# A four-layer graph network on one core: layer 0's table first in the prologue, layer 2's sums with one-hot weights

## The chip, the core and the metric

The kernel runs on one core of a Trainium2 chip. The core has five engines, each with its own instruction queue that is worked through in order: TensorE (PE in the profile, with its weight loads as PEld), VectorE (DVE), ScalarE (ACT), GpSimd (POOL) and SyncE (SP), which here only issues transfers. Transfers run on 16 DMA engines. The time is device microseconds from start to end; each version is run several times and the median counts.

## The reference, cut

There are 12500 nodes with 128 features and 212500 edges, sorted by destination. Four layers follow one another; each normalises the nodes, applies a ReLU, gathers a row for each edge's source, works on it, and adds it up at the edge's destination.

```python
edge_index = jnp.stack([src, dst])
h = jnp.maximum(_layernorm(x, axis=-1), 0.0)
x = x + _L0_gnn_ref(h, edge_index, edge_attr_16, ...)   # attention over 4 heads
h = jnp.maximum(_layernorm(x, axis=-1), 0.0)
x = x + _L1_gnn_ref(h, edge_index, edge_weight1, ...)   # weighted sum, then a dense layer
h = jnp.maximum(_layernorm(x, axis=-1), 0.0)
x = x + _L2_gnn_ref(h, edge_attr_9, edge_index, L2_gnn_weights)
h = jnp.maximum(_layernorm(x, axis=-1), 0.0)
x = x + _L3_gnn_ref(h, ...)                             # mean over neighbours, two dense layers, batch norm
return x
```

The two layers that the change touches, in their core:

```python
def _L0_gnn_ref(h, edge_index, edge_feat, W, W_e, a, ln_scale, ln_bias):
    Wh = (h @ W.T).reshape(N, H, D)
    Wh_src = Wh[src]
    Wh_dst = Wh[dst]
    attn = (jnp.concatenate([Wh_src, Wh_dst], axis=-1) * a[None]).sum(-1)
    ...
    agg = jax.ops.segment_sum(alpha[..., None] * Wh_src, dst, num_segments=N)

def _L2_gnn_ref(features, edge_sh, edge_index, weights):
    x1 = _split(features[src], IRREPS_IN)      # 32 scalars and 32 vectors of 3
    x2 = _split(edge_sh, IRREPS_SH)            # 1 + 3 + 5 numbers for each edge
    for p, (i1, i2, io) in enumerate(PATHS):   # five paths
        tmp = jnp.einsum('eui,ej,ijk->euk', x1[i1], x2[i2][:, 0, :], CG[p])
        msg = jnp.einsum('euk,uw->ewk', tmp, weights[p]) * alpha
        ...
    return out.at[dst].add(msgs)
```

Left out of the first are the leaky ReLU, the edge term and the softmax over the edges of one destination, which gives `alpha`. In layer 2 the products `tmp` (352 numbers for each edge: 128 + 128 + 96) depend on the edge; the mixing by `weights` doesn't. So the products may be summed at the destinations first and mixed afterwards.

## The kernel before

**Windows of edges.** The edges are cut into 208 groups of 1024 (128 partitions by T = 8). Since they are sorted, a group's destinations lie in a window of 128 nodes that begins at the group's smallest destination. The sum over a group is a matmul with a one-hot matrix (edge by node of the window), and it is added to an accumulator `acc.t`, a ring of 2048 + 128 node columns in SBUF. When all groups of a batch of four node blocks (512 nodes, 25 batches) are in, a "node" generator takes the batch out of the ring, finishes the layer for it and stores the next layer's table to DRAM. Rows are fetched by `gather` (L659 to L662): eight indirect transfers for each group, issued by POOL.

**Order.** Outside of blocks marked `manual_schedule` the framework orders each engine's instructions by the place in the program and by when their inputs are expected; inside the blocks (the four layers' loops) each engine follows the program's order.

**Prologue.** First constants. Then the edge preparation (L221 to L333): `di` and `si` are loaded by `load_edges`, a padded copy `dpad` goes through DRAM and comes back as `seq`; VectorE works out each window's base and relative index, with 70-odd small fills of `least` and `end` (L277 to L291), and POOL reduces over partitions (L253). Then the weights: `WE`, layer 0's weight with the attention vectors folded in (L343 to L358), `WeB`, `TP` (layer 2's mixing matrix, L371 to L380) and `mixer`. Last, in the pool p0 (L919 to L953), layer 0's table: for each of 25 batches a load of `x`, the normalisation (`norm`: statistics on VectorE, root on ScalarE, scaling on VectorE), ReLU on ScalarE, four transposes, a copy, four matmuls with `WE`, copies out by ScalarE (`tt`, 132 columns for each node) and VectorE (`sd`, the destination's part, split into three bf16 parts `s3`), and two stores, to `tab0` and `sdt`. All buffers there are two deep.

**Layer 0** (L958 to L1137) gathers from `tab0`; each window's rows `X` lie in one of 15 buffers and are used for the logits in the same step and, LAG = 7 steps later, for the messages `msg` (L1078) and their sum.

**Layer 2** (`layer2` and the block behind it, L1282 to L1370). For each window, `window2` is a generator with these stages: eight scalings by ScalarE (`A`, L1307); the one-hot `S` by VectorE (L676); the products `B` and `C` by VectorE (L1314 to L1326); 24 matmuls into `pag` with the products as weights and `S` streamed, so that the sums stand with products on partitions and nodes in columns, and two copies `R` (L1328 to L1335); three matmuls with `TP` into `po`, the mixing (L1339); the addition of `po`, 128 columns, to the ring (L1342). `step` calls keep three windows under way: in step g VectorE does `S`, `B` and `C` of window g and then the addition of window g-3, while TensorE sums window g-1 and mixes window g-2. X has 11 buffers. `node2` transposes the batch's four blocks (L533), clears them in the ring (L535) and goes on to layer 3's table.

`window2` also serves a general path at the end of the program that doesn't run with these inputs.

Of the kernel before, what the change touches and what calls it, by code (L numbers as in the profile page):

```python
# [14 lines left out]
F = mybir.dt.float32  # L15
I = mybir.dt.int32
B16 = mybir.dt.bfloat16
# [9 lines left out]
P = 128  # L27
# [66 lines left out]
def gnn_kernel(ctx: ExitStack, tc, x, src, dst, ef16, ef9, ew, W0, We0, a0, lns, lnb, W1, b1,  # L94
# [101 lines left out]


    si = cst.tile([P, NG, T], I, name="si")
    rel = cst.tile([P, NG, T], F, name="rel")
# [4 lines left out]
    relc = cst.tile([P, NW, NT], B16, name="relc")  # L204
    early = ExitStack()
    tmp = early.enter_context(tc.tile_pool(name="acp", bufs=1))
    wslot = tmp.tile([P, NW, NT], F, name="wslot")
# [6 lines left out]
    NSG = NG // SG  # L214
    NK = -(-NB // NBK)

# [4 lines left out]
    with tc.tile_pool(name="ed", bufs=1) as ep:  # L221
# [54 lines left out]
        least = ep.tile([P, NG], F, name="least")  # L276
        vec.memset(least, 0.0)  # L277
        for k, g in enumerate(done):
            if g + 1 < NG:
                vec.memset(least[:, g + 1 :], float(min(NBK * P * (k + 1), N)))  # L280
        vec.memset(least[:, G0:], float(W0_ * P))
        for k, g in enumerate(done):
            if g + 1 >= G0 and g + 1 < NG:
                vec.memset(least[:, g + 1 :], float(min(NBK * P * (k + 1), N)))
        vec.tensor_tensor(least, base, least, ALU.is_lt)

        end = ep.tile([P, NG], F, name="end")
        vec.memset(end, float(RW - W))
        for k, g in enumerate(done):
            if g + 6 < NG:  # L290
                vec.memset(end[:, g + 6 :], float(NBK * P * (k + 1) + RW - W))  # L291
        vec.tensor_tensor(end, base, end, ALU.is_gt)
# [44 lines left out]

    WE = cst.tile([P, P + 2 * H], F, name="WE")
    W1T = cst.tile([P, P], F, name="W1T")
    WlT = cst.tile([P, P], F, name="WlT")  # L340
    WrT = cst.tile([P, P], F, name="WrT")
    with tc.tile_pool(name="wt", bufs=2) as wp, tc.tile_pool(name="wtp", bufs=2, space=PSUM) as pp:
        for w, to in ((W0, WE[:, :P]), (W1, W1T), (Wl, WlT), (Wr, WrT)):  # L343
            wn = wp.tile([P, P], F, name="wn")
            nc.sync.dma_start(wn, w)
            wps = pp.tile([P, P], F, name="wps")
            pe.transpose(wps, wn, ident)
            vec.tensor_copy(to, wps)
            if w is W0:
                ab = wp.tile([P, 2 * H], F, name="ab", bufs=1)  # L350
                vec.memset(ab, 0.0)
                for h in range(H):
                    for s in range(2):
                        nc.sync.dma_start(ab[h * HD : (h + 1) * HD, s * H + h : s * H + h + 1],
                                          a0[h : h + 1, s * HD : (s + 1) * HD].rearrange("o d -> d o"))
                aps = pp.tile([P, 2 * H], F, name="aps", bufs=1)
                pe.matmul(aps, wn, ab, start=True, stop=True)
                vec.tensor_copy(WE[:, P:], aps)  # L358
    WeB = cst.tile([P, T * H], F, name="WeB")
# [65 lines left out]
    acc = SimpleNamespace(t=None, ring=RW)  # L425
    tab0 = dram.tile([N, P + H], F, name="tab0")
    sdt = dram.tile([AW, 3 * H], B16, name="sdt")
    lgt = dram.tile([TOT, H], F, name="lgt")
# [32 lines left out]
    def cols(k, j=0, n=NBK):  # L461

        c = k * NBK * P if acc.ring is None else k * NBK * P % acc.ring
        return slice(c + j * P, c + min(j + n, NB - k * NBK) * P)

    def settle(k):

        if acc.ring is not None and k and k * NBK * P % acc.ring == 0:
            vec.tensor_tensor(acc.t[:, :W], acc.t[:, :W], acc.t[:, acc.ring :], ALU.add)
            vec.memset(acc.t[:, acc.ring :], 0.0)  # L470

# [54 lines left out]
    def node2(sp, pp, k, split=True):  # L526
# [5 lines left out]
        for j in range(nb):  # L532
            pe.transpose(po[:, j, :], acc.t[:, cols(k, j, 1)], ident)  # L533
        yield
        vec.memset(acc.t[:, cols(k)], 0.0)  # L535
        vec.tensor_tensor(xv[:, :, :HD], xv[:, :, :HD], po[:, :, :HD], ALU.add)
# [381 lines left out]

    WN = P + 2 * H  # L919
    with tc.tile_pool(name="p0", bufs=2) as sp, tc.tile_pool(name="p0p", bufs=2, space=PSUM) as pp:  # L920
        zs = sp.tile([P, 3 * H], B16, name="zs", bufs=1)
        vec.memset(zs, 0.0)
        for r in range(N, AW, P):
            n = min(P, AW - r)
            nc.sync.dma_start(sdt[r : r + n, :], zs[:n, :])
        for b0, nb in batches(4):
            xt = sp.tile([P, nb, D], F, name="xt")
            load_rows(xt, x, b0, nb)
            h = sp.tile([P, nb, D], F, name="h0")
            for _ in norm(sp, xt, nb, h):  # L930
                pass
            pt = pp.tile([P, nb, P], F, name="pt")
            for j in range(nb):
                pe.transpose(pt[:, j, :], h[:, j, :], ident)
            hT = sp.tile([P, nb, P], F, name="hT")
            act.copy(hT, pt)
            pw = pp.tile([P, 2, 512], F, name="pw")
            pwv = pw[:, :, : 2 * WN].rearrange("p a (c n) -> p a c n", n=WN)
            for j in range(nb):
                pe.matmul(pwv[:, j // 2, j % 2, :], hT[:, j, :], WE, start=True, stop=True)  # L940
            tt = sp.tile([P, nb, P + H], F, name="tt")
            sd = sp.tile([P, nb, H], F, name="sd")
            for a in range(0, nb, 2):
                act.copy(tt[:, a : a + 2, :], pwv[:, a // 2, : min(2, nb - a), : P + H])
                vec.tensor_copy(sd[:, a : a + 2, :], pwv[:, a // 2, : min(2, nb - a), P + H :])

            s3 = sp.tile([P, nb, 3, H], B16, name="s3")
            for k in range(3):
                vec.tensor_copy(s3[:, :, k, :], sd)
                if k < 2:  # L950
                    vec.tensor_tensor(sd, sd, s3[:, :, k, :], ALU.subtract)
            store_rows(tab0, tt, b0, nb, P + H)
            store_rows(sdt, s3.rearrange("p j k h -> p j (k h)"), b0, nb, 3 * H)  # L953

    acc.t = tmp.tile([P, RW + W], F, name="acc")
    H1 = H + 1
    vec.memset(acc.t, 0.0)
    with (tc.tile_pool(name="e0", bufs=2) as sp, tc.tile_pool(name="e0p", bufs=2, space=PSUM) as pp,  # L958
# [322 lines left out]

    def layer2(sp, pp, deep=4):  # L1282
        feats = feature_stream(ef9f, 9, 4, "ef", sp)
# [19 lines left out]
        def window2(reg, got, r, b, nodes):  # L1303
            X, e, Y = got
            A = sp.tile([P, T, P], F, name="A")
            for t in range(T):
# [5 lines left out]
            v3 = [P, T, 3, HD]  # L1312
            B = sp.tile([P, T, 4, HD], F, name="B")
            vec.tensor_tensor(B[:, :, :3, :], X[:, :, None, :HD].to_broadcast(v3),  # L1314
# [3 lines left out]
            vec.tensor_reduce(B[:, :, 3, :], V.rearrange("p t k u -> p t u k"), AX.X, ALU.add)  # L1318
            C = sp.tile(v3, F, name="C")
            part = pp.tile(v3, F, name="part", bufs=1)  # L1320
            for i in range(3):
# [3 lines left out]
                if i:  # L1325
                    vec.tensor_tensor(part if i == 1 else C, part, o, ALU.add)  # L1326
            yield
            pag = pp.tile([P, 3, W], F, name="pag", bufs=1)  # L1328
            for c, f in enumerate((A, B, C)):
                for t in range(T):  # L1330
                    lhs = f[:, t] if c == 0 else f[:, t].rearrange("p k u -> p (k u)")
                    pe.matmul(pag[: TPK[c] * HD, c, :], lhs, S[:, t, :], start=t == 0, stop=t == T - 1)  # L1332
            R = sp.tile([P, 3, W], F, name="R")
# [6 lines left out]
            yield  # L1340
            win = ds(reg.load(b, AW - W if acc.ring is None else acc.ring - 1), W)
            reg.end(vec.tensor_tensor(acc.t[:, win], acc.t[:, win], po, ALU.add))  # L1342
# [3 lines left out]
    with (tc.tile_pool(name="e2", bufs=3) as sp, tc.tile_pool(name="e2p", bufs=2, space=PSUM) as pp,  # L1346
          tc.tile_pool(name="n2", bufs=2) as ns, tc.tile_pool(name="n2p", bufs=1, space=PSUM) as np_):
        rows2, mix, _, window2 = layer2(sp, pp, 11)
        nodes = Nodes(lambda k: node2(ns, np_, k), 4)
# [5 lines left out]

        with tc.manual_schedule():
            mixed[0] = mix(0)
            g = -1
            while nodes.step(g := g + 1) or g < NG + 3:
                if g + 1 < NG:  # L1360
                    mixed[g + 1] = mix(g + 1)
                if g < NG:
                    going[g] = window2(reg2, (rows2(si[:, g, :]), *mixed.pop(g)), rel[:, g, :],
                                       bir[0:1, g : g + 1], widx[:, g : g + 1])
                    step(g)
                step(g)
                step(g)
                step(g - 3)
                step(g - 1)
                step(g - 2)  # L1370
# [394 lines left out]
```

## Time and profile before

| what | us |
|---|---|
| median of 3 runs | 7448.18 |
| the runs | 7453.02, 7439.46, 7448.18 |
| the profiled execution | 7429.66 |
| its span, first to last instruction | 7427.8 |
| layer 0: first and last gather of POOL | 231.9 and 2416.3 |
| layer 1: first gather | 2525.0 |
| layer 2: first gather | 3900.6 |
| layer 3: first gather | 6016.7 |

In the page, busy times are sums over the engine's instructions. A line of the groups reads: line of the program, engine, operation, what it writes and reads, shapes, count; then busy time and the mean of one; then the engine's idle time ahead of them and who ended it. A line of the timeline reads: start, duration, engine, line, operation; a bracket at its end gives the idle time ahead of it. Matmuls in fp32 show as two instructions each. PEclk is the TensorE clock that was granted, as a share of full speed.

### The profile page before, as it was taken

Reading aid. Unit: us, or ns where it says so; the run is one execution under the profiler, and the core shown is the slowest. Engines: PE = TensorE matmul, PEld = TensorE weight load, DVE = VectorE, ACT = ScalarE, POOL = GpSimd, SP = SyncE. Lnnn points to the kernel's source line nnn. Section 1 sums busy time; section 2 is a strip of 40 time slices with the busy share of each in tenths; the row PEclk is TensorE's granted clock in tenths of the full one; section 3 lists DMA queues with packets and bytes.
Section 4 is the critical chain, followed back from the end, with each engine's and each line's share of the span. In section 5 each row is a group of like instructions: output and inputs, shape, how many; then the busy total and the mean of one; then the engine's idle time right before and its main releaser. Section 6 shows DMA issues by size and latency. Waiting matters only on the chain.

```text
span 7427.8 us, 119421 instructions
## 1 busy us (share of the span) xinstructions
PE 5056.1 (68%) x39957; PEld 3687.5 (50%) x39958; DVE 5283.1 (71%) x10506; ACT 2841.6 (38%) x7693; POOL 5145.2 (69%) x5372
## 2 busy tenths in 40 slices
PE   3344445444444499888987787778787758788787
PEld 2344444344444366555656777777777732222222
DVE  5678888888888445544448999999999944545454
ACT  1244444444444234434443333333333314444443
POOL 0577777777775377777737777777777767777772
PEclk8566666666666699999987888888888868888887
DMA  5444444444443433333322222222222244344333
GB/s 84 96 105 103 104 106 105 107 106 103 105 105 94 84 88 96 95 90 94 93 72 57 67 71 66 68 69 67 70 69 66 69 126 105 105 106 105 102 103 108
DMA packets 741279, 674.54 MB, mean 91 GB/s; under 512 B 341283, under 2 KB 629398, under 8 KB 740631
## 3 DMA queue, kind: packets, MB, share of 16 engines
q0 software_dynamic: 186624, 382.17, 21.4%
q1 hardware_dynamic: 554027, 284.63, 15.0%
q8 instruction: 316, 5.18, 0.3%
q14 instruction: 312, 2.56, 0.1%
HBM read 603.91 MB, written 63.28 MB: 90 GB/s over the span
## 4 chain that ended last, share of the span: by engine, by line
PE 26%; POOL 16%; DVE 10%; issue 9%; DMA 3%; ACT 1%; DVEq 1%; SPq 0%; POOLq 0%; ACTq 0%
POOL X L661 15%; PE pw L1181 5%; PE px L1200 5%; PE px L1443 4%; PE pw L1429 4%; PE pag L1275 3%; PE pg L1544 3%; DMA X<-htab,si 2%; DVE oh L680 1%; POOL X L669 1%; DVEq L692 1%; PE pag L1332 1%; DVE oh L676 1%; DVE f L1536 1%; DVE B L1314 1%
## 5 line engine op out<-in xcount | busy, mean ns | idle before, releaser
L661 POOL DMA_INDIRECT X<-tab,si x1664 | 1635.6, 983 | 531.0 <-issue 473.0
L661 POOL DMA_INDIRECT X<-htab,si x1664 | 1574.0, 946 | 533.7 <-issue 509.7
L669 POOL DMA_INDIRECT xg<-tab,si x968 | 919.7, 950 | 358.9 <-issue 127.3
L669 POOL DMA_INDIRECT X<-htab,si x968 | 937.1, 968 | 324.2 <-issue 83.8
L1082 PE MATMUL pag<-oh,msg 128*128 128x128 f32 x3328 | 670.5, 383 | 357.4 <-DVE msg L1078 328.7
L1082 PEld LDWEIGHTS pag<-oh,msg 128*128 128x128 f32 x3328 | 620.3, 288 | 373.7 <-DVE msg L1078 336.5
L1454 ACT CAST xb<-px 128x384 bf16<-128x384 f32 x1050 | 501.3, 478 | 737.4 <-PE px L1443 722.0
L1212 ACT ACTIVATE xs<-px,wslot 128x128 f32<-128x128 f32 x1050 | 382.6, 367 | 774.7 <-PE px L1200 698.2
L1332 PE MATMUL pag<-oh,A 128*128 128x128 f32 x3328 | 561.4, 341 | 0.0
L1544 PE MATMUL pg<-xg,oh 128*128 128x385 bf16 x968 | 370.9, 388 | 256.4 <-DVE f L1537 194.9
L1275 PE MATMUL pag<-oh,X 128*128 128x128 f32 x1936 | 432.6, 309 | 165.5 <-DVE acc L1268 121.6
L1332 PEld LDWEIGHTS pag<-oh,A 128*128 128x128 f32 x3328 | 543.5, 256 | 0.0
L1181 PE MATMUL pw<-ohb,xs 128*128 128x128 f32 x2100 | 541.3, 342 | 0.0
L1307 ACT ACTIVATE A<-X,ef 128x128 f32<-128x128 f32 x1664 | 509.9, 391 | 15.7 <-DMA X<-htab,si 15.4
L676 DVE TENSOR_TENSOR oh<-iop,rel 128x1024 f32<-128x1024 f32 (+1 forms) x321 | 388.7, 1211 | 163.2 <-PE pg L1544 162.7
L1200 PE MATMUL px<-tabS,oha 128*32 128x128 f32 x8652 | 488.1, 299 | 5.8 <-ACT xs L1212 5.8
L1071 ACT ACTIVATE oh<-iop,far 128x128 f32<-128x128 f32 x1664 | 451.6, 382 | 48.9 <-DVE ohj L879 38.7
L1181 PEld LDWEIGHTS pw<-ohb,xs 128*128 128x128 f32 x2100 | 334.4, 200 | 219.8 <-issue 218.0
L1334 ACT COPY R<-pag 128x256 f32<-128x256 f32 x208 | 77.4, 372 | 955.6 <-PE pag L1332 955.6
L1332 PE MATMUL pag<-oh,B 128*128 128x128 f32 x3328 | 437.8, 288 | 0.0
L1275 PEld LDWEIGHTS pag<-oh,X 128*128 128x128 f32 x1936 | 326.3, 212 | 206.6 <-DVE acc L1268 139.6
L1332 PEld LDWEIGHTS pag<-oh,B 128*128 128x128 f32 x3328 | 427.3, 208 | 0.0
(460 smaller groups left out, 10444.9 us busy)
## 6 DMA issues: line engine op xcount, KB each, us to landing
lob<-lo SPq DMA_DIRECT2D x252, 224.0 KB
rb<-rel SPq DMA_DIRECT2D x208, 256.0 KB
X<-htab,si POOLq DMA_INDIRECT x2632
X<-tab,si POOLq DMA_INDIRECT x1664
xtab<-xv SPq DMA_DIRECT2D x72, 256.0 KB
xv<-xtab SPq DMA_DIRECT2D x72, 256.0 KB
xg<-tab,si POOLq DMA_INDIRECT x968
lob<-lo SPq DMA_DIRECT2D x84, 160.0 KB
```

What stands on the lines that cost most here:

```text
L661: pool.indirect_dma_start(out=t[:, s, :], out_offset=None, in_=table[:, :], in_offset=bass.IndirectOffsetOnAxis(ap=idx[:, s : s + 1], axis=0))
L669: pool.indirect_dma_start(out=ts[-1][:, : table.shape[1]], out_offset=None, in_=table[:, :], in_offset=bass.IndirectOffsetOnAxis(ap=idx[:, ...
L676: vec.tensor_tensor(s, iop[:, None, :].to_broadcast([P, T, W]), r[:, :, None].to_broadcast([P, T, W]), ALU.is_equal)
L1071: act.activation(S[:, t, :], iop, AF.Abs, bias=far[:, t : t + 1])
L1082: pe.matmul(pag, msg[:, t, :], S[:, t, :], start=t == 0, stop=t == T - 1)
L1181: pe.matmul(pw, x, b, start=j == 0, stop=j == NT - 1)
L1200: pe.matmul(px[q * SL : (q + 1) * SL, :], a[:, jj * P + q * SL : jj * P + (q + 1) * SL], tabS[:, blk, :], start=True, stop=True)
L1275: pe.matmul(p, r[t], s[:, t, :], start=t == 0, stop=t == T - 1)
L1307: act.activation(A[:, t, :], X[:, t, :], AF.Copy, scale=e[:, t, 0:1])
L1332: pe.matmul(pag[: TPK[c] * HD, c, :], lhs, S[:, t, :], start=t == 0, stop=t == T - 1)
L1454: act.copy(x[:, : 3 * P], px)
L1544: pe.matmul(p, s[:, t, :], r[t], start=t == 0, stop=t == T - 1)
```

## The change

**Part 1, the prologue.** `tab0`, `sdt`, `WE` and the pool p0 move ahead of the edge preparation. Eight loads of `x` are issued first, ahead of `W0` and the attention vectors, and a ninth buffer keeps the loads eight batches ahead. For each batch the scaling by VectorE is gone: ScalarE does scaling, shift and ReLU in one instruction for each block, four for a batch. `tt` is copied by VectorE instead of ScalarE, two copies for a batch. The destination's part goes to `sdall`, for all blocks; its split into three and its store to `sdt` come once, after the loop. p0's buffers are three deep.

**Part 2.** The fills of `least` and `end`, and the first clearing of the ring, go from VectorE to POOL.

**Part 3, layer 2.** The products of a window lie in one tile `prods` of 352 columns. `S` is now the weight and the products are streamed: 8 matmuls of 352 columns where there were 24 of 128. The sums come out with nodes on partitions; one copy `R` follows, then three transposes into `pT`, and the addition of 3 x 128 columns to a ring `acc2` of three parts. The mixing with `TP` moves from the window (three matmuls) to `node2` (12 matmuls for a batch of four blocks, in place of four transposes); the clearing of the ring there is three times as wide. `acc2` is cleared at the start of layer 2. The number of stages of the generator and their order stay.

```diff
+    sp, pp = (pre.enter_context(p) for p in (tc.tile_pool(name="p0", bufs=3),
+                                             tc.tile_pool(name="p0p", bufs=2, space=PSUM)))
+    xs0 = {}
+
+    def rows0(k):
+        if k < NK:
+            b0, nb = k * NBK, min(NBK, NB - k * NBK)
+            xs0[k] = sp.tile([P, nb, D], F, name="xt", bufs=9)
+            load_rows(xs0[k], x, b0, nb)
+
+    NK = -(-NB // NBK)
+    for k in range(8):
+        rows0(k)
...
+        nc.sync.dma_start(wn, W0)
...
+    for k in range(NK):
+        b0, nb = k * NBK, min(NBK, NB - k * NBK)
+        xt = xs0.pop(k)
...
+        act.activation(rs, mv[:, :, 1], AF.Sqrt, bias=eps)
+        vec.reciprocal(rs, rs)
+        mr = sp.tile([P, nb], F, name="mr")
+        vec.scalar_tensor_tensor(mr, mv[:, :, 0], -1.0, rs, op0=ALU.mult, op1=ALU.mult)
+        h = sp.tile([P, nb, D], F, name="h0")
+        for j in range(nb):
+            act.activation(h[:, j, :], xt[:, j, :], AF.Relu, bias=mr[:, j : j + 1], scale=rs[:, j : j + 1])
...
+            vec.tensor_copy(tt[:, a : a + n, :], pw[:, :n, : P + H])
+            vec.tensor_copy(sdall[:, b0 + a : b0 + a + n, :], pw[:, :n, P + H :])
+        store_rows(tab0, tt, b0, nb, P + H)
+        rows0(k + 8)
+
+    s3 = sp.tile([P, NB, 3, H], B16, name="s3", bufs=1)
+    for k in range(3):
+        vec.tensor_copy(s3[:, :, k, :], sdall)
...
+    store_rows(sdt, s3.rearrange("p j k h -> p j (k h)"), 0, NB, 3 * H)
...
-        vec.memset(least, 0.0)
+        pool.memset(least, 0.0)
...
-    vec.memset(acc.t, 0.0)
+    pool.memset(acc.t, 0.0)
...
         for j in range(nb):
-            pe.transpose(po[:, j, :], acc.t[:, cols(k, j, 1)], ident)
-        yield
-        vec.memset(acc.t[:, cols(k)], 0.0)
+            if not split:
+                pe.transpose(po[:, j, :], acc.t[:, cols(k, j, 1)], ident)
+            for c, q in enumerate(TPK if split else ()):
+                pe.matmul(po[:, j, :], acc.t[: q * HD, c, cols(k, j, 1)], TP[: q * HD, c, :], start=c == 0, stop=c == 2)
+        yield
+        vec.memset(acc.t[..., cols(k)], 0.0)
...
-            A = sp.tile([P, T, P], F, name="A")
+            prods = sp.tile([P, T, SK], F, name="prods")
+            A, B, C = prods[:, :, :P], prods[:, :, P : 2 * P], prods[:, :, 2 * P :]
...
+            if late:
+                pag = pp.tile([P, SK], F, name="pag", bufs=1)
+                for t in range(T):
+                    pe.matmul(pag, S[:, t, :], prods[:, t, :], start=t == 0, stop=t == T - 1)
+                R = sp.tile([P, SK], F, name="R")
+                act.copy(R, pag)
+                yield
+                for c, q in enumerate(TPK):
+                    pe.transpose(pT[: q * HD, c, :], R[:, c * P : c * P + q * HD], ident)
+                yield
+                win = ds(reg.load(b, RW - 1), W)
+                reg.end(vec.tensor_tensor(acc.t[:, :, win], acc.t[:, :, win], pT, ALU.add))
+                return
...
+        acc.t = sp.tile([P, 3, RW + W], F, name="acc2", bufs=1)
+        rows2, mix, _, window2 = layer2(sp, pp, 11, True)
...
         with tc.manual_schedule():
+            vec.memset(acc.t, 0.0)
```

## The prediction

> **What bounds the kernel now.** I read the busy time by stage first (engines, granted clock, DMA share, GB/s; columns as in its header).
>
> ```profile
> core 0: us, PE busy (x) PEld busy (x) DVE busy (x) ACT busy (x) POOL busy (x), PEclk, DMA share, GB/s
> ...
> 34.00:80.00 46.00, 6.59 (x15) 2.80 (x15) 33.67 (x87) 0.00 (x0) 1.57 (x1) 1.00 0.27 89
> ...
> 100.00:231.00 131.00, 76.39 (x294) 59.79 (x294) 81.74 (x493) 50.32 (x125) 0.20 (x1) 0.58 0.45 102
> 300.00:2300.00 2000.00, 921.21 (x6655) 836.45 (x6654) 1678.29 (x3624) 856.01 (x2312) 1526.97 (x1553) 0.64 0.44 104
> 4000.00:5900.00 1900.00, 1511.85 (x10911) 1421.18 (x10912) 1769.73 (x2305) 633.90 (x2176) 1437.06 (x1520) 0.87 0.26 68
> ```
>
> In layer 2 (last line) VectorE is busiest, 93%, but POOL issues 1520 gathers in 1900 us, one each 1.25 us. The timeline tells who leads:
>
> ```profile
> 5050.14 0.94 POOL L661 DMA_INDIRECT X<-htab,si  x1 [0.30 <-issue]
> ...
> 5050.59 1.22 DVE L676 TENSOR_TENSOR oh<-iop,rel 128x1024 f32<-128x1024 f32 x1
> ...
> 5052.92 0.95 DVE L1314 TENSOR_TENSOR B<-X,py 128x768 f32<-128x768 f32 x1 [1.11 <-PE py L1297]
> ```
>
> Counted in eights, the gather of 5050.14 is the last of window 114, whose B is the one at 5052.92: 1.8 us behind its end. In windows without a batch of nodes ahead B follows at 1.7 to 1.8 us and VectorE has waited for it; after a batch it is up to 3.4 behind and catches up. So VectorE waits for rows, POOL sets the period: 8 x 1.249 = 9.99 us, 208 times.
>
> In layer 0 it is otherwise. The last gather starts at 2416.31, but the last message product only at 2491.88. For window 0 the message product comes 67 us behind its gather (308.6 against 241.9), for window 200 131 us (2434.2 against 2303.0): VectorE's side takes 10.63 us a window and POOL 10.30. Layer 0 ends by its consumers, and they start with the first ST.
>
> The prologue, from the same timeline:
>
> ```profile
> 1.27 15.61 SPq L128 DMA_DIRECT2D si<-in_src_dram  x1
> ...
> 16.93 14.59 SPq L136 DMA_DIRECT2D di<-in_dst_dram  x1
> ...
> 99.91 0.38 SPq L158 DMA_DIRECT2D xt<-in_x_dram  x1
> ...
> 159.67 0.58 ACT L936 COPY hT<-pt 128x512 f32<-128x512 f32 x1 [0.99 <-PE pt L934]
> ...
> 162.57 0.38 ACT L944 COPY tt<-pw 128x264 f32<-128x264 f32 x1 [2.12 <-issue]
> 162.85 0.63 ACT L455 ACTIVATE h<-h 128x512 f32<-128x512 f32 x1
> ...
> 164.74 0.58 ACT L936 COPY hT<-pt 128x512 f32<-128x512 f32 x1 [0.99 <-PE pt L934]
> ...
> 231.89 1.29 POOL L661 DMA_INDIRECT X<-tab,si  x1 [18.97 <-DVE cut_s L975]
> ...
> 238.43 0.52 DVE L1004 TENSOR_SCALAR ST<-rb,pcol 128x1024 bf16<-128x1024 bf16 x1 [7.28 <-DMA rb<-rel]
> ```
>
> The table's first load waits until 99.9, behind the whole edge preparation. Then each batch takes 5.07 us (hT to hT), 25 x 5.07 = 127. It is a loop through ScalarE's queue: hT, matmuls, tt, the next batch's ReLU behind that tt, transposes, hT. No engine is full: VectorE 81.74 of 131 us.
>
> **Part 1 and 2, the prologue.** VectorE's work up to 231 is 10.57 (first 34 us) + 33.67 + 9.36 (80 to 100) + 81.74 = 135.3 us. Removed, from the groups: the scaling L451 28.0, the splits L949 12.3 and L951 8.6, the fills 3.4 + 3.2 + 1.0 and the ring's 1.9: together 58.4. Added: 49 copies of 264 columns, at 0.42 (128x256 from PSUM, L520) 20.6; 25 small operations at 0.17 (L448) 4.3; five splits of 392 columns at 0.39 (L1029, 448 columns) 2.0: together 26.9. Left: 103.8 us. ScalarE: four ReLUs of 128 columns at 0.31 (eight of L1307 in 2.45) where one took 0.63, and two tt copies of 0.38 less, so 2.1 us a batch; TensorE as before, 1.11 + 2.18 at the low clock. Nothing there needs 5 us a batch, and the loop through ScalarE is cut, since tt is VectorE's now.
>
> The fills on POOL, some 60 at up to 0.2 us, fall into the 50 us that it waits for L251 ahead of L253; without that cover they would cost 12. The ring's clearing on POOL stands ahead of the first gather: at L157's 0.2 us for 128 columns 3.5 us, against an engine that waited 19 there.
>
> SP is passed by many issues. Eight loads of x (0.4 each), W0 and eight pieces of the vectors (0.33 + 3.98) come first, some 8 us; then si and di, whose two entries hold the queue for 15.61 + 14.59 us. I take it that the table's stores and later loads stand behind them: SP is free at about 39. With tt three deep the table gets three batches far by then, at 2.7 us of VectorE each; with the small rest say 12 of the 103.8 us are done. 92 are left. At VectorE's best, without a gap, they end at 131; at the share it reached in the table stage (81.74 / 131 = 62%) at 187. The edge preparation alone had 73% (33.67 / 46). Two independent streams fill each other's gaps, so I take 85%: 108 us, ending at 147. In the run before, the table's last VectorE work lay 12 us ahead of the first ST (226.5 to 238.4: last stores, the padding, rb); kept, that gives 159, a gain of 79 us. Bounds: 131 + 12 gives 95; 187 + 12 gives 39; with si and di out of the way altogether, 104 + 5 + 12 = 121 gives 117.
>
> The gain passes through layer 0 because its consumers set its end; layers 1 to 3 shift with it. POOL may lead by more at first, but X has 15 buffers, 155 us at 10.3, and a stall of POOL there costs nothing while its lead lasts.
>
> **Part 3, layer 2.** VectorE, per window:
>
> ```profile
> L1342 DVE TENSOR_TENSOR acc<-acc,po 128x128 f32 x189 | 52.4, 277 | 0.4 <-issue 0.4
> ...
> L538 DVE TENSOR_TENSOR xv<-xv,pn 128x384 f32<-128x384 f32 x22 | 11.9, 541 | 0.0
> L535 DVE MEMSET acc<- 128x512 f32 x22 | 10.7, 485 | 3.8 <-DVE acc L1342 3.8
> ...
> L536 DVE TENSOR_TENSOR xv<-xv,pn 128x128 f32<-128x128 f32 x22 | 5.0, 228 | 0.0
> ```
>
> The wider addition: 384 against 128 columns differ by 0.31 (L538, L536); at most three of the old ones, +0.55. I take 0.30, the nearer row. The clearing: L470 (128 columns, 165 ns) and L535 give 0.83 ns a column, so 1536 columns take 1.34, +0.85 a batch, +0.10 a window. Together +0.40 (bounds 0.36 and 0.65). VectorE's idle time is 1900 - 1769.7 = 130 us in 190 windows, 0.69 a window: it hides. Bare it would be 0.40 x 208 = 83 us.
>
> TensorE: 48 instructions of 128 streamed columns become 16 of 352, 8% fewer columns, and 32 weight loads go. The sums took (511 + 400 + 362) / 190 = 6.7 us of busy time a window; I take 6.1. Bounds: 5.4 (16 x 352/128 x 0.1225, from 16 in 1.96 us) and 11.3 (136 columns in 0.27 at half clock, L940). Three transposes at 0.31 (L1294) for a mixing of 1.2; 24 instructions at 0.3 a batch where four stood: +6 us, +0.7 a window. Sum 7.96 - 0.6 - 0.3 + 0.7 = 7.8 of 9.99 us: no gain and no loss, as POOL leads.
>
> A rule speaks against that. In this trace TensorE at 46% busy (layer 0) was granted 0.64 of its clock, and 16 instructions of 128 columns took 3.77 us at one time and 2.04 at another; in layer 2 at 80% it was granted 0.87. The Trainium skill (TensorE: Matmul & The Clock Gate, Part 1 and Part 4) says that an idle window of about 3.4 us halves the clock and that transposes don't count as activity as matmuls do. By it the sparser TensorE of the new layer 2 could stay at half speed, by the row it keeps most of the clock. Since a slowed TensorE has no gaps left, I go by the row.
>
> At the start the clearing of 6528 columns (5.4 us) lies in VectorE's wait of 15.4 us ahead of its first B at 3912. At the end two batches of nodes and three additions follow the last gather: some +4 us (0 to 10).
>
> **Sum.** 7429.7 - 79 + 4 = 7355 on the profiled execution, which lies 18.5 under the median; on the median 7448 - 75 = 7373.
>
> **Rivals.**
> A. The prologue's queues block one another: in-order VectorE stands on edge work whose data come late, and the table keeps its 62%. For it: si and di hold SP for 30 us, and VectorE idles 18.7 us ahead of L226 before. Against: two streams. 39 - 4 = 35 us gained: 7413.
> B. VectorE becomes the bound in layer 2, slower in sum. Place: A, B and C share one tile. If B of a window then waited for ScalarE's A, whose eight start 0.8 us behind the one-hot and take 2.45, VectorE would lose 2.1 us a window: 9.99 - 0.69 + 0.40 + 2.1 = 11.8, +1.8 x 208 = 375: 7748. It decides from 0.29 (free margin) + 75/208 = 0.65 us a window. Against: the columns are disjoint, and before, different columns of B were written without a wait.
> C. TensorE at half clock is the bound: 11.3 + 0.9 + 0.9 + 0.9 = 14 us a window, +830. Against: layer 1 at 89% busy was granted 0.93.
> D. The gain is lost in layer 0, because its first windows wait for something else: 7448 + 4.
>
> **How the numbers follow.** Forecast 0.70, own range 7331 to 7419 (gains 117 and 39, costs 0 to 10); A 0.14; B 0.08; C 0.04; D 0.04. Forecast and A hold 0.84, so the range is theirs, a little wider for the estimate of SP's order: 7325 to 7425. A change under 0.2%, 15 us, can't be told from none. Faster 0.84, same 0.04, slower 0.12.
>
> **What would show it.** Right: first ST near 159, the first gather no later, batches at 3 to 4 us; layer 2 at 9.99 us a window with VectorE near 97%. Wrong: gathers of layer 2 more than 1.25 us apart, B's wait naming ScalarE, or an idle VectorE beyond 60 us.

## The result and the profile after

The changed kernel takes 7386.03 us (median of 4 runs, 7376.58 to 7390.43), the kernel before 7443.82 (4 runs, 7430.93 to 7453.02): a ratio of 0.9927 with a 95% interval of 0.9914 to 0.9940, 58 us less. The prediction was 7373, range 7325 to 7425. The profiled execution takes 7387.41 us with a span of 7385.5; the one before had 7427.8 (7429.66 us, below the lowest of its four runs), so the two spans differ by 42 us and the medians by 58. Times of single stages are compared below, not these totals.

Busy time by stage, columns as in the header (PEclk is the granted clock, DMA share the mean busy share of 16 DMA engines; it goes over 1 where the recorded times of packets overlap):

```profile
core 0: us, PE busy (x) PEld busy (x) DVE busy (x) ACT busy (x) POOL busy (x), PEclk, DMA share, GB/s
16.00:118.00 102.00, 56.03 (x292) 44.45 (x291) 66.80 (x307) 53.52 (x138) 9.95 (x64) 0.76 0.99 157
118.00:179.00 61.00, 7.61 (x19) 3.45 (x19) 20.80 (x128) 0.27 (x1) 5.51 (x6) 0.50 0.74 32
...
118.00:141.00 23.00, 1.41 (x4) 0.66 (x4) 8.70 (x43) 0.00 (x0) 0.43 (x1) 0.50 1.61 14
...
4000.00:5900.00 1900.00, 1405.58 (x4729) 876.35 (x4729) 1837.14 (x2320) 618.04 (x1984) 1436.65 (x1523) 0.86 0.26 68
```

The first two rows are the prologue. In the first, VectorE is busy 65% and the DMA engines are full. In the second, nothing computes for long: VectorE has 20.8 of 61 us, and the DMA engines move 32 GB/s. In its first 23 us (third row) they are full with only 14 GB/s: the rows of `sdt` are pieces of 24 bytes. The timeline of the changed kernel's prologue says what goes on (start, duration, engine, line, operation; in brackets the idle time ahead):

```profile
16.33 0.40 SPq L128 DMA_DIRECT2D di<-in_dst_dram  x1
19.30 15.12 SPq L150 DMA_DIRECT2D tab<-tt  x3
...
49.13 0.37 SPq L128 DMA_DIRECT2D si<-in_src_dram  x1
50.31 17.45 SPq L150 DMA_DIRECT2D tab<-tt  x3
...
117.89 23.03 SPq L150 DMA_DIRECT2D sdt<-s  x2
...
127.35 0.15 DVE L402 CAST rough<-worst 128x1 int32<-128x1 f32 x1
...
141.42 13.49 SPq L411 DMA_DIRECT2D rel<-rl  x13
...
145.07 0.49 DVE L410 CAST rl<-prl 128x128 bf16<-128x128 f32 x2 [17.56 <-DMA rel<-rl]
...
161.57 0.29 DVE L425 COPY WrT<-wps 128x128 f32<-128x128 f32 x1 [1.88 <-PE wps L424]
...
172.93 0.43 SPq L1019 DMA_DIRECT2D rb<-rel  x1
```

Twice the stores of the table stand behind a load of edges, `di` at 16.3 and `si` at 49.1, for 15.1 and 17.5 us. VectorE's last work for the table is over at 117.9, where the one store of `sdt` begins to hold SP for 23 us. VectorE has done the table and the edge work at 127.4, and then waits 17.6 us for the first stores of `rel16` (the relative indices, in bf16) to land. Thirteen of them follow one another, then the three weights, then the mixing matrix on VectorE until 171.3. The first rows of `rel16` have to be loaded back (`rb`), and the first `ST`, the one-hot matrix with which VectorE begins layer 0, starts at 178.8. Before, it was 238.4.

The 59.6 us pass through layer 0 unchanged: the last message product comes at 2432.3 where it came at 2491.9. Behind it the lead over the kernel before is 58.8 us at layer 1's first gather, 50.1 at the end of layer 1's last full batch, 43.6 at layer 2's first gather, 43.8 at layer 3's and 42.3 at the end.

Layer 2, the groups of its stage from 4000 to 5900 us (busy, mean ns, idle ahead and who ended it). The first line is VectorE's first product in the kernel before, the others are of the changed kernel:

```profile
L1314 DVE TENSOR_TENSOR B<-X,py 128x768 f32<-128x768 f32 x190 | 180.5, 950 | 91.2 <-PE py L1297 38.9 <-PE py L1294 29.9 <-issue 10.8
...
L1372 PE MATMUL pag<-prods,oh 128*128 128x352 f32 x3038 | 1120.9, 531 | 0.0
...
L1356 DVE TENSOR_TENSOR prods<-X,py 128x768 f32<-128x768 f32 x189 | 178.8, 946 | 18.4 <-issue 15.6 <-PE py L1337 2.0 <-PE py L1334 0.8
...
L1380 DVE TENSOR_TENSOR acc<-acc,pT 128x384 f32 x190 | 103.5, 545 | 0.4 <-issue 0.4
...
L604 DVE MEMSET acc<- 128x1536 f32 x23 | 30.8, 1338 | 8.9 <-DVE acc L1380 8.9
```

The gathers of the stage, before and after (shortest, median and longest in ns, then the first and the last start):

```profile
L661 POOL DMA_INDIRECT X<-htab,si x1664: 940/944/1363, 3900.5 to 5980.5; - x185
...
L730 POOL DMA_INDIRECT X<-htab,si x1664: 940/944/1311, 3856.9 to 5934.2; - x185
```

They still come every 1.25 us. From first to last gather layer 2 takes 2077.3 us where it took 2080.0, and from its first gather to layer 3's 2116.0 where it took 2116.2. VectorE's wait ahead of `B` has shrunk from 91.2 to 18.4 us: the added work went into that wait. At layer 2's start something was lost. The timeline of the changed kernel there:

```profile
3839.05 0.18 DVE L513 RECIPROCAL rs<-rs 128x4 f32<-128x4 f32 x1 [4.12 <-ACT rs L511]
...
3842.23 5.50 DVE L1412 MEMSET acc<- 128x6528 f32 x1 [1.85 <-ACT t L523]
3847.65 0.36 DVE L586 TENSOR_TENSOR o<-pn,b_b 128x256 f32<-128x256 f32 x1
...
3853.35 0.79 SPq L150 DMA_DIRECT2D htab<-t  x2
3856.93 0.96 POOL L730 DMA_INDIRECT X<-htab,si  x1 [33.57 <-issue]
```

The clearing of `acc2` stands on VectorE ahead of the last, short batch of layer 1 (L586 on), whose table rows are stored at 3853.4 and which the first gather waits for. From the reciprocal of the last full batch to the first gather it takes 17.9 us; before it was 11.4.

### The profile page after: what moved, and what is told of

The parts are those of the page before. It is cut to its first block, busy times and chain, and to the rows that moved or that the text cites. A ratio compares the mean times of both kernels' runs of the same rounds, so it can differ in the third digit from the quotient of the medians.

```text
span 7385.5 us, 105557 instructions
## 1 busy us (share of the span) xinstructions
PE 4921.2 (67%) x33167; PEld 3072.3 (42%) x33168; DVE 5326.5 (72%) x10302; ACT 2837.0 (38%) x7509; POOL 5151.4 (70%) x5434
## 4 chain that ended last, share of the span: by engine, by line
## 5 line engine op out<-in xcount | busy, mean ns | idle before, releaser
L1372 PE MATMUL pag<-prods,oh 128*128 128x352 f32 x3328 | 1231.2, 532 | 0.0
L1372 PEld LDWEIGHTS pag<-prods,oh 128*128 128x128 f32 x3328 | 733.0, 226 | 409.3 <-issue 176.7
L1350 ACT ACTIVATE prods<-X,ef 128x128 f32<-128x128 f32 x1664 | 509.9, 390 | 15.4 <-DMA X<-htab,si 15.1
L1374 ACT COPY R<-pag 128x352 f32<-128x352 f32 x208 | 94.1, 452 | 856.8 <-PE pag L1372 856.8
L1499 PE MATMUL px<-tabS,oha 128*32 128x384 bf16 x4326 | 422.2, 378 | 0.2
L1036 PE MATMUL pt<-WeB,eT 128*128 128x32 f32 x416 | 112.3, 359 | 458.1 <-ACT eT L1034 455.7
```

Source lines behind the costliest of these rows:

```text
L1350: act.activation(A[:, t, :], X[:, t, :], AF.Copy, scale=e[:, t, 0:1])
L1372: pe.matmul(pag, S[:, t, :], prods[:, t, :], start=t == 0, stop=t == T - 1)
L1499: pe.matmul(px[q * SL : (q + 1) * SL, :], a[:, jj * P + q * SL : jj * P + (q + 1) * SL], tabS[:, blk, :], start=True, stop=True)
```

## The experiments

They ran in three series, each on a chip of its own. On the chips of the first two series the kernel before takes 10189 and 10195 us, on that of the third 7435, which is like that of the result; so every ratio is one to the kernel before on the same chip. The prologue hardly differs between chips. With the changed kernel's prologue left as it is, the first `ST` comes at 178.8 us on the result's chip, at 180.5 on that of the first series, at 175.9 and 176.4 on that of the second, and at 180.5 and 181.3 on that of the third: within 1 us on one chip, within 6 over all.

### The parts alone

Parts 1 and 2 alone: `layer2`, the node step and `settle` (it adds the end of the ring to its start) as before.

```diff
-        rows2, mix, _, window2 = layer2(sp, pp, 11, True)
+        rows2, mix, _, window2 = layer2(sp, pp, 11)
```

> The changed kernel with layer 2 (and its node step) as before, so parts 1 and 2 alone. Theory: the new layer 2 costs some 11 us, 6.4 at its start (the offset between the two profiles goes from -50.1 to -43.6 us over the 5.50 us clearing of acc2) and 5 at its end (-44.7 to -39.7), and gains nothing between. So first ST stays at 179 us, the layer 1 to 2 transition is 6 us and the layer 2 to 3 transition 5 us shorter than in the changed kernel, and the time is 7386 - 11 = 7375. Rival: the offsets drift by themselves from run to run and part 3 is free: 7386.

Measured: 10131.45 against 10189.18, ratio 0.9944 (0.9927 to 0.9961), first `ST` at 180.5.

Part 3 alone: the kernel before with the new layer 2.

```diff
+        acc.t = sp.tile([P, 3, RW + W], F, name="acc2", bufs=1)
-        rows2, mix, _, window2 = layer2(sp, pp, 11)
+        rows2, mix, _, window2 = layer2(sp, pp, 11, True)
```

> The kernel before with the new layer 2 alone (part 3). Theory: first ST stays at 238 us, layer 2 keeps 9.99 us a window, and the two transitions cost 6 + 5 us: 7444 + 11 = 7455. Rival 1, part 3 is free: 7444. Rival 2, part 3 brings part of the gain (more than the 60 us of the prologue are needed to explain it): below 7440.

Measured: 9963.60, ratio 0.9777 (0.9755 to 0.9799), first `ST` at 239.7. The control of the second series, the changed kernel unaltered:

> The changed kernel itself, unaltered, as the control on the chip of this series. On a chip like that of the result it runs 58 us under the kernel before (7386 against 7444). On one like that of the first series, where the kernel before took 10189 us and TensorE's results came late in layer 2, it should stand where the two halves measured there add up: -58 (parts 1 and 2) and -226 (part 3) give a ratio of 0.972.

Measured: 9884.17 against 10194.74, ratio 0.9693 (0.9676 to 0.9709).

So the prologue brings 58 us there, as much as the whole change on the result's chip, and part 3, which I had put at a loss of 11, brings 226. The product of the two ratios is 0.972; the control's 0.9693, on another chip, agrees with it within the intervals. Neither expectation foresaw that, since they came from a chip on which layer 2 is paced otherwise. On a chip like the result's the parts were not run alone; there the split is read from the trace. Part 2 was not parted from part 1 anywhere. On the slower chip, the waits of layer 2 with the old form (parts 1 and 2 alone, from 5300 to 7800 us; sum, times, longest):

```profile
ACT R L1364 <- remote: 1194.9, 117, 112.6
...
POOL X L726 <- ACT A L1337: 784.5, 162, 12.3
...
DVE acc L1372 <- remote: 742.9, 158, 5.6
```

and one window of its timeline:

```profile
6526.58 0.83 PE L1369 MATMUL po<-R,TP 128*128 128x128 f32 x6
...
6532.94 0.29 DVE L1372 TENSOR_TENSOR acc<-acc,po 128x128 f32 x1 [3.02 <-remote]
```

("remote" is a releaser that the profile doesn't find on this core.) The instructions named read results of TensorE: `R` the sums, the addition the mixing. The mixing is recorded as over at 6527.4, and the addition of its result starts at 6532.9, with VectorE idle for the last 3 us. The copy `R` starts 2.9 us (median) behind the recorded end of the matmuls ahead of it, against 0.1 in the kernel before on the result's chip. With the new form it is uneven: most copies start 0.1 behind, but more than a third over 1 us, up to 11.9. A window takes 14.2 us with the old form (first to last gather 2947.9 us in 207 windows), 13.1 with the new one (2710.3), while POOL, whose gather takes the same 0.95 us, waits for `X` to come free. The clock granted in layer 2 is 0.74 and 0.76 (over the whole run 0.706 and 0.710), against 0.87 before and 0.86 after on the result's chip (0.789 and 0.783).

I take it that TensorE's results, which come later than the records say, set the window there. The new form streams 8% fewer columns and has 8% shorter windows, which fits; but it also has one copy `R` in place of two, and no run on these chips varied the columns alone, so it is not shown. The lower clock may be part of it or not; no run parts the two. Why these chips are slower was not found.

### Does the store of sdt set the end of the prologue?

Its store in five parts, and its store by ScalarE instead of SP:

```diff
+        if k % 5 == 4 or k == NK - 1:
...
+            store_rows(sdt, s3[:, c0:c1].rearrange("p j k h -> p j (k h)"), c0, c1 - c0, 3 * H)
```

> The changed kernel with the splits and the store of sdt in five parts, one after every fifth batch, instead of one at the end. Theory (order of SP's queue): the one store holds SP for 23.03 us from 117.89 on, ahead of the 13 stores of rel16; without it these start near 118 and all behind them comes 20 to 23 us earlier: first ST at 157 to 160 us, time 7386 - 20 = 7366. Rival (the transfers themselves are full): the 12500 pieces of 24 bytes need their 23 us of the DMA engines in any case, and they are at 8 to 9 tenths busy from 10 to 115 us: the table's stores and the edge loads come later by as much, first ST at 174 to 185, time 7380 to 7390.

```diff
-    store_rows(sdt, s3.rearrange("p j k h -> p j (k h)"), 0, NB, 3 * H)
+    store_rows(sdt, s3.rearrange("p j k h -> p j (k h)"), 0, NB, 3 * H, nc.scalar)
```

> The changed kernel with the one store of sdt issued by ScalarE, which has nothing behind it there until layer 0 starts, instead of SP. Theory (order of SP's queue): the 13 stores of rel16 go out from 118 us on beside it, first ST at 157 to 162 us, time 7386 - 18 = 7368. Rival (transfers full): the rel16 stores share the engines with the pieces of sdt and land hardly earlier, first ST at 172 to 179, time 7380 to 7386.

Measured: first `ST` at 180.0 and 176.8, where the unaltered prologue has 180.5 on the same chip (parts 1 and 2 alone) and 175.9 in the control on the other; ratios 0.9711 (0.9692 to 0.9730) and 0.9706 (0.9687 to 0.9724), no better than the control (0.9693 on its chip). A gain of some 20 us was expected, and none or 4 came: both times the rival holds. With five parts VectorE waits 43.7 us for stores of the table, where it waits 21.0 with the unaltered prologue on that chip. The timeline with the store on ScalarE's queue:

```profile
116.03 0.43 SPq L485 DMA_DIRECT2D bet_c<-in_L_gnn_beta_dram  x1
124.33 28.19 SPq L411 DMA_DIRECT2D rel<-rl  x13
...
139.58 0.29 DVE L410 CAST rl<-prl 128x128 bf16<-128x128 f32 x1 [12.45 <-DMA rel<-rl]
```

SP is free at 116.5 and issues the first `rel16` stores at 124.3, but VectorE still waits until 139.6 for one to land. From 118 to 141 us the DMA engines move 18 GB/s at a share of 1.69: they, and not SP's queue, are taken by the 12500 pieces of 24 bytes. My theory of the queue's order fell here.

### Are the small pieces of the edge loads what holds the table?

`di` and `si` are loaded with a group in a row, 4 KB in one piece, and turned on TensorE:

```diff
-        load_edges(di, dst, 0, NG, N, 1)
-        load_edges(si, src, 0, NG, 0, 1)
...
+                nc.sync.dma_start(raw[:, 0, :], v[: HG * GE].rearrange("(g e) -> g e", e=GE))
+                nc.sync.dma_start(raw[: HG - 1, 1, :], v[HG * GE : NF * GE].rearrange("(g e) -> g e", e=GE))
...
+                            pe.transpose(ps[:, q, :], r[:, :, t + q], ident[:HG, :HG])
+                        vec.tensor_copy(to[:, k * HG : (k + 1) * HG, t : t + 4], ps.rearrange("p q g -> p g q"))
```

> The changed kernel with di and si loaded in pieces of 4 KB (a group in a row) and turned on TensorE, in place of 26500 pieces of 32 bytes each; VectorE does some 6.5 us more. Theory (the transfers of small pieces set the prologue): the stretches in which di and si fill the DMA engines (19 to 34 and 50 to 68 us, 32 us together) go, and first ST comes 20 to 32 us earlier, 147 to 159 us. Rival (VectorE's in-order queue sets it): first ST moves by under 8 us, or later by its 6.5 us.

Measured: first `ST` at 174.4, ratio 0.9693 (0.9675 to 0.9711). On this chip the unaltered prologue has 175.9 and 176.4. That looks like the rival, but the DMA view and VectorE's timeline of that run show another thing. In the stretch from 58 to 64 us (40 equal slices):

```profile
DMA  0000000000000000000000014834999541000000
GB/s 27 27 27 27 27 27 27 27 27 27 0 27 27 27 27 27 27 27 27 27 27 27 27 61 140 150 113 143 294 345 294 160 143 41 27 27 27 27 27 27
```

and on VectorE:

```profile
44.27 0.43 DVE L261 COPY tt<-pw 128x264 f32<-128x264 f32 x1 [13.20 <-DMA tab<-tt]
...
70.58 0.43 DVE L261 COPY tt<-pw 128x264 f32<-128x264 f32 x1 [12.97 <-DMA tab<-tt]
```

The load of 103 rows moves at a steady 27 GB/s with the DMA engines all but idle (from 58 to 60 us a share of 0.06, one engine of 16), and the table's stores stand behind it on the same queue. The stall had only changed its cause. The Trainium skill (DMA: Bandwidth & Descriptors, "Why a DMA increments its semaphore by 16 and not by 1") says that a transfer is spread over the largest number of engines up to 16 that divides its slowest dimension on both sides. 103 is prime, so by it that would be one engine, which agrees with the 0.06. With 103 rows cut into 96 and 7 (and the other load, of 104, into 96 and 8):

```diff
+                for k, n in ((0, HG), (1, HG - 1)):
+                    for a, b in ((0, 96), (96, n)):
+                        nc.sync.dma_start(raw[a:b, k, :], v[(k * HG + a) * GE : (k * HG + b) * GE]
```

> As f4_loads, but the loads of 103 rows are cut into 96 and 7. In f4_loads the 32-byte pieces were gone and the DMA engines half idle, yet VectorE stood twice for 13 us on a table store, because the loads of 103 rows moved at 27 GB/s (one engine's rate) and everything on SP's queue stood behind them. Theory (transfers set the prologue, the loads of f4_loads were slow in another way): without those stalls first ST comes at 147 to 160 us against 175.9 of the control. Rival (VectorE's in-order queue and the tail behind the edge work set it): 168 to 176, as in f4_loads (174.4).

Measured: first `ST` at 152.4, 28 us ahead of the unaltered prologue on the same chip (180.5 and 181.3), inside the theory's range; 7352.39 against 7434.96, ratio 0.9884 (0.9868 to 0.9901). In its prologue:

```profile
16.00:98.00 82.00, 52.39 (x326) 41.07 (x325) 72.41 (x326) 54.62 (x140) 11.89 (x65) 0.89 0.96 196
98.00:152.00 54.00, 7.71 (x19) 3.52 (x19) 20.12 (x124) 0.27 (x1) 4.90 (x5) 0.50 0.45 31
```

VectorE is busy 88% of the first row, though it has some 5 us more to do, and the DMA engines move 196 GB/s where they moved 157. The second row, the tail behind the last edge work, has hardly changed: the store of `sdt`, then `rel16`, the weights and the mixing matrix. From the first store of `rel16` to the first `ST` it takes 37.0 us, where it took 37.4.

### The tail and the clearing

Thirteen buffers for the `rel16` stores in place of two:

```diff
-                rl = ep.tile([P, P], B16, name="rl", bufs=2)
+                rl = ep.tile([P, P], B16, name="rl", bufs=13)
```

> The changed kernel with 13 buffers rl instead of 2, so that the 13 stores of rel16 don't wait for one another to land. Theory (the end of the prologue is a chain behind the transfers of sdt): their 13.49 us shrink to the 0.4 us of an issue each, some 5 us, and first ST comes 7 to 9 us earlier, at 170 to 172 us; time 8 us under the control. Rival (VectorE's order): the stretch is filled by other late work, first ST at 177 to 179.

Measured: first `ST` at 168.7, 7.2 us ahead of the control, as the theory has it; the stores take SP 6.24 us, but still begin behind the 22 us of `sdt`. The time, 7 us under the control, ratio 0.9687 (0.9661 to 0.9714), can't be told from it.

`acc2` cleared by POOL:

```diff
-            vec.memset(acc.t, 0.0)
+            pool.memset(acc.t, 0.0)
             mixed[0] = mix(0)
```

> The changed kernel with acc2 cleared by POOL instead of VectorE at the start of layer 2. Theory: the 5.50 us clearing stands on VectorE ahead of the last batch of layer 1, whose table store the first gather waits for; on POOL, idle until then, it costs nothing: from the last batch's update to the first gather it is 5 to 6.5 us shorter, time 5 to 6 us under the control. Rival: the clearing is hidden, the offset has another cause: no change; or POOL's clearing ends late and delays the first gather: no change or +5.

Measured: ratio 0.9689 (0.9672 to 0.9706), not to be told from the control. The place itself can be: from the reciprocal of the last full batch to the first gather it takes 10.5 us. In the ten profiled runs with the clearing on VectorE, on all chips, it takes 17.3 to 17.9, and with the old layer 2 11.4 and 11.9. So the clearing costs some 6.5 to 7.4 us where it stands. POOL clears while VectorE goes on:

```profile
5206.07 5.54 POOL L1412 MEMSET acc<- 128x6528 f32 x1 [17.50 <-ACT g L576]
5207.27 0.42 DVE L586 TENSOR_TENSOR o<-pn,b_b 128x256 f32<-128x256 f32 x1
```

### What paces layer 2

Fewer columns on TensorE (the sums over `C` are left out), and one more reduction on VectorE:

```diff
-                    pe.matmul(pag, S[:, t, :], prods[:, t, :], start=t == 0, stop=t == T - 1)
+                    pe.matmul(pag[:, : 2 * P], S[:, t, :], prods[:, t, : 2 * P], start=t == 0, stop=t == T - 1)
```

> The changed kernel with 256 of the 352 product columns streamed in layer 2: the sums over the products C are left out. Theory (on these chips TensorE's pace is what layer 2 waits for, 13.8 us a window): a quarter of the streamed columns goes, 16 x 96 of some 7000 a window, so 2.5 to 3.5 us a window, layer 2 500 to 700 us shorter (2882 to about 2250), time near 9250. Rival (the chip is slow in something else, a wait for rows or for semaphores): layer 2 under 100 us shorter.

```diff
             vec.tensor_reduce(B[:, :, 3, :], V.rearrange("p t k u -> p t u k"), AX.X, ALU.add)
+            if late:
+                vec.tensor_reduce(B[:, :, 3, :], V.rearrange("p t k u -> p t u k"), AX.X, ALU.add)
```

> The changed kernel with one more reduction of 0.96 us on VectorE in each window of layer 2. If TensorE's pace binds there (13.8 us a window against 9.7 of VectorE): no change, under 40 us. If VectorE stands on the path (it waits for a result and the next step waits for it): up to 0.96 x 208 = 200 us longer. The wider addition and clearing of the change, 0.4 us a window, are hidden by the same cover.

This series met a chip like that of the result, where TensorE's results come at once, so the condition of both theories, a TensorE that sets the pace, was not given. (Their 13.8 us a window and 2882 us are also more than the control's 13.0 and 2699.4.) Measured: without the columns of `C` 7381.92, ratio 0.9931 (0.9915 to 0.9948), layer 2 in 2077.1 us from first to last gather: the same as the changed kernel (0.9927, 2077.3). TensorE's columns cost nothing there. So the step "no gain and no loss, as POOL leads" holds for TensorE. What the columns cost on the slower chips is left open by this run.

The extra 0.96 us on VectorE: 7557.83, ratio 1.0172 (1.0155 to 1.0189), 176 us above the kernel without the columns of `C`, which stands for the changed kernel on the same chip. Of its 200 us (0.96 x 208) 24 were hidden. The medians are uncertain by some 12 us each, but the profiled executions say the same: from layer 2's first gather to layer 3's 2290.2 us against 2116.1, so 26 hidden. That is 0.12 us a window. Of VectorE's waits in the stage from 4000 to 5900 us there is nothing left but the hand-over from the addition to the clearing:

```profile
DVE acc L604 <- DVE acc L1382: 8.1, 21, 0.4
DVE acc L1382 <- issue: 0.8, 4, 0.2
```

The changed kernel has these:

```profile
DVE prods L1356 <- issue: 15.6, 25, 0.8
DVE acc L604 <- DVE acc L1380: 8.9, 23, 0.4
...
DVE acc L1380 <- issue: 0.4, 2, 0.2
```

They sum to 28 us with the two left out (2.8), 0.15 a window. That, not the 63 us that 1900 - 1837 leaves, is about what more work can use; the rest lies between instructions that wait for nothing by name.

### Together

Loads of 96 and 7 rows, `sdt` in five parts, 13 buffers `rl`, the clearing by POOL.

> The edits that gained or should gain, together: loads as in g1_loads16, sdt's store in five parts, 13 buffers rl, acc2 cleared by POOL. If they add up: first ST at 135 to 150 us (control 175.9), the transition from layer 1 to 2 some 8 us shorter, time 35 to 50 us under the control, a ratio to the kernel before of 0.965 (control 0.9693). If sdt's pieces in the middle hold the table back as in e3_sdt_five: first ST at 150 to 165, ratio 0.967.

Measured: 7343.53, ratio 0.9883 (0.9867 to 0.9900), no better than the loads alone. The clearing's place takes 10.6 us, 7 less, and the `rel16` stores 6.17 us instead of 13.53, but first `ST` is at 153.8: VectorE waits 18.1 us in sum for the table's stores where it waited 1.2. I put that down to the parts of `sdt` between them, as in the run with five parts alone; they take back what was won. This kernel and the one with the loads alone both beat the changed one, by 0.4% (0.9884 against 0.9927, intervals apart). The loads with `rl` and the clearing, but `sdt` whole, would have been the next to try; it was not run.

## Why the prediction was right, and where its steps were not

| step | predicted | measured |
|---|---|---|
| VectorE's work for the prologue, in all | 103.8 us | 99.8 |
| of it done at 39 us | 12 us | 21.3 |
| its share from there on | 85% | 59% (78.5 of 132.6 us) |
| its end | 147 us | 171.4 (table and edge work alone 127.4) |
| from the table's last VectorE work to the first ST | 12 us | 60.9 |
| first ST | 159 us | 178.8 |
| gain through layer 0 | whole | whole (59.6 of 59.6) |
| layer 2, a window | 9.99 us | unchanged (2077.3 against 2080.0 in sum) |
| wider addition, clearing of a batch | 0.577, 1.34 us | 0.545, 1.338 |
| TensorE's sums, in all | 6.1, 7.8 us a window | 5.9, 7.4 |
| acc2's clearing | hidden | 6.5 us |
| layer 2's tail | +4 us | +2.5 (36.2 to 38.7 between the last gather and layer 3's first), taken back by 2.7 less between the gathers |

**The forecast held, with its main term 20 us too large.** The gain of the prologue was put at 79 us and measured at 59.6. The step that failed is this one: "In the run before, the table's last VectorE work lay 12 us ahead of the first ST ...; kept, that gives 159". It was not kept: it is 60.9 us now. Before, the stores of `rel16`, the weights and the mixing matrix stood ahead of the table (the stores at 67.6 us) and were over before its first load. With the table moved forward they are the tail, and with them the store of `sdt`, which was spread over 25 batches and is one now. I had counted what the move issues earlier and not asked what it leaves last.

In the terms of the sum it is the 85% that was too high. From 34 to 118 us VectorE reached 71% (59.6 of 84 us), but behind 127.4 only 11.9 of 44 us, and over the whole stretch 59%, less than the 62% of rival A. That first `ST` still came 20 us ahead of rival A's 199 is due to other terms: VectorE had done 21.3 us of its work at 39, where I had 12, and 7.4 us passed from its end to the first `ST`.

**Rival A's mechanism was half there.** VectorE did stand on the table's stores, 20.9 us in all, behind `di` and `si`, and the run with the loads of 96 and 7 rows shows what the loads in small pieces cost: 28 us. The two did not hold SP for 30 us on end as I had assumed, since `si` was issued at 49.1. I had taken the loads to hold SP; the runs with `sdt` show that a full set of DMA engines holds back the stores on SP's queue even when the small pieces come from ScalarE's.

The range of 100 us holds both the forecast and rival A, and 59.6 lies halfway between their 79 and 39, so that the time fell inside it does not tell them apart; the trace does. There is luck in the point, too: on the profiled executions it missed by 32 us, on the medians by 13, because the profiled execution before was fast for its kernel and the one after was not. And the chip was one like that of the trace; on one of the slower ones the change gains 310 us (9884.17 against 10194.74).

**Layer 2** went by the steps, except that the clearing at the start, "in VectorE's wait of 15.4 us ahead of its first B", was not put there by the order of instructions but ahead of layer 1's last batch, where someone waited. The cover for the 0.40 us was really there, and it was nearly all there was: I took 0.69 us a window from the busy times, of which the waits by name were 0.50 (94.6 us in 190 windows), and 0.12 to 0.15 is left. Rivals B and D were not seen.

**Rival C and the clock rule.** On the result's chip the row decided rightly: the clock granted in layer 2 is 0.86 after and 0.87 before, with TensorE busy 74% instead of 80%. The Trainium skill's rule on idle time and transposes (TensorE: Matmul & The Clock Gate, Parts 1 and 4) did not come to bear there. But what rival C described, a TensorE that sets the window at 14 us, is what the two slower chips look like (14.2 before, 13.1 after), and there the change gains in layer 2 instead of losing. Nothing in the trace I predicted from shows such a chip.

Summed up on the profiled executions, 7387.4 stands where 7355 was forecast. 19 us of the 32 are the prologue, 6.5 the clearing, and 4 go back because I had added 4 for layer 2's end, and layer 2 with its end takes as long as before (2116.0 against 2116.2). The rest, 11, lies in layers whose code is the same: 9.5 between the end of layer 0 and layer 1's last full batch, 1.5 in layer 3. In the six profiled executions on this kind of chip, layer 1 from its first gather to that batch takes 1363.3 to 1373.0 us with the same code, 1364.2 in the one before and 1373.0 in the one after; so the 9 us are of the size by which executions differ.

## What to carry to other kernels

When work is moved forward, list what stood ahead of it before: that is the new tail, and nothing is left to run beside it. For a stage that is full of small transfers, count pieces and rows before queues: changing the queue moved at most 4 us where 20 were expected, while pieces of 4 KB brought 28 us, once the loads were cut so that they spread over the engines. Cover was here what the waits by name add up to, not the span less the busy time.

## What the runs showed of the hardware

- Some 26500 loaded pieces of 32 bytes held the DMA engines for 14 to 17.5 us, 12500 stored pieces of 24 bytes for 22 to 24, whether SP or ScalarE issued them.
- A load of 103 rows of 4 KB moved at 27 GB/s with one engine's share of the 16 busy; cut into 96 and 7 rows it held nothing up.
- The same program took 7435 us on one chip and 10190 on others. VectorE's and POOL's instructions were as long; the copy of a sum started 2.9 us (median) behind the recorded end of its matmuls in layer 2's old form, against 0.1.
- Layer 2's new form was worth nothing between the gathers on one kind of chip (2077.3 against 2080.0 us, and a quarter of the streamed columns less made no difference) and 2.2% of the whole on another (0.9777).
- In layer 2, TensorE busy 80%, 74% and 64% (the last with the quarter left out) was granted 0.87, 0.86 and 0.81 of its clock.
